# Layer-0 feed-forward of a two-layer ViT tower: tokens of seven quads turned by VectorE block transposes and DRAM transfers instead of PE transposes

## The chip, the core and the metric

The kernel runs on one core of one Trainium2 chip. The metric is the device time of one execution in microseconds (us); the time before is the median of three runs, 1921.87 us (1919.85 to 1925.09). The engines of the core are PE (matrix multiply), ACT, DVE (VectorE) and POOL (GpSimd). SP is a queue whose work here is to issue DMA transfers. Each engine works through its own instructions in order, and waits on semaphores for the others.

## What is computed

32 images of 256 tokens with 256 features, in float32, go through a tokenizer, a layer 0 (attention, then a feed-forward part that only half of the tokens get), and a layer 1. The change lies in the feed-forward part of layer 0, which in the reference, cut to what matters, is:

```python
def _L0_ffn_ref(x, attention_mask, wr, br, w1, b1, w2, b2):
    weights = (jnp.einsum('bsd,do->bso', x, wr) + br)[..., 0]
    k = max(1, int(CAPACITY * s))            # 128 of 256 tokens
    kk = k - 1 if k > 1 else 1               # 127 are processed
    _, idx = jax.lax.top_k(weights, k)
    sel_idx = idx[:, :kk]
    sel = jnp.take_along_axis(x, sel_idx[:, :, None], axis=1)
    h = jax.nn.gelu(jnp.einsum('bkd,dh->bkh', sel, w1) + b1)
    y = jnp.einsum('bkh,hd->bkd', h, w2) + b2
    ...
    processed = jnp.zeros_like(x).at[batch_idx, sel_idx].set(y)
    return processed + x
```

The product with `w1` sums over the features, so PE needs the selected tokens with features on the partitions. They arrive with tokens on the partitions; somebody has to turn them.

## The kernel before

The program is one long stream, stage after stage: tokenizer (A), layer-0 attention by pairs of images (B), layer-0 feed-forward by quads, that is four images (C), layer-1 attention by pairs (D), layer-1 feed-forward by images (E). In A to D the order of instructions on each engine is written by hand: what the Python loop calls first is first in every engine's queue. No scheduler moves anything there.

During B the tokens of each image are ranked and scattered by rank to DRAM (`ranked`, line 401, indirect DMAs of POOL). Stage C handles eight quads u = 0 to 7 in steps t, four steps to a quad. `ORDER_C` (line 857) says at which step, relative to t = 4u, each piece of quad u is called; within one step the pieces are called in the order of the tuple, whichever quad they belong to:

- `first_ranks` (line 220, step -8): four DMAs of SP load the first 128 ranked tokens of each image into `cs`, tokens on the partitions, 128 x 4 x 256. There are two `cs` buffers.
- `turn_c` (line 225, step -1): 8 PE transposes of 128x128 by the identity (line 230) into two PSUM banks, which ACT (k = 0, line 194) and DVE (k = 1, line 196) copy to `xsel`, 128 x 2 x 512, features on the partitions. There is one `xsel` buffer.
- `hidden_c` (line 814, steps 0 and 1): 16 matmuls of 512 columns from `xsel`, in two halves, with the Gelu on ACT (line 821). Float32 matmuls show in the trace as two instructions each, so 32 for a quad.
- `made` (line 823, steps 2 and 3): per half, 16 matmuls of 256 columns (32 in the trace), for two images; DVE adds the bias for each image (line 829, `cy`), and SP stores the result to DRAM (line 830, `results`).
- `fetch` (line 832, steps 4 and 5) is POOL's indirect DMAs from `results`; `update` (line 843, steps 5 and 6) adds on DVE (line 849) and takes statistics (lines 124 and 125).

So around the end of quad u-1 the calls run: step 4u-2: `made` of quad u-1, first half; `update` of quad u-2, second half. Step 4u-1: `turn_c` of quad u; `made` of quad u-1, second half. Step 4u: `hidden_c` of quad u. The weight products of `prepare()` (from line 630), one piece at the end of each step from t = 8, are set between these; they put PE work into some steps and none into others. Quad 0 is turned by a direct call of `turn_c` at the end of stage B (line 536).

All PE matmuls go through one helper and have line 116 in the profile; transposes of `turn_c` have line 230.

Of the kernel before, what the change touches and what calls it, by code (L numbers as in the profile page):

```python
# [33 lines left out]
F32 = mybir.dt.float32  # L34
# [6 lines left out]
P = 128  # L41
# [39 lines left out]
def vit_tower(tc, a, out):  # L81

    nc = tc.nc
# [13 lines left out]
    def bank():  # L97
        return ppool.tile([P, 512], F32, name="bank", tag="bank")

    def col(name, i=0):  # L100
        c = COLS[name][0] + i
        return cols[:, c : c + 1]
# [12 lines left out]
    def mm(o, lhsT, rhs, first=True, last=True):  # L115
        nc.tensor.matmul(o, lhsT, rhs, start=first, stop=last)  # L116
# [4 lines left out]
    def stats(st, i, c, x):  # L121

        six = spool.tile([P, 6], F32, name="six")
        nc.vector.bn_stats(six, x)  # L124
        nc.vector.bn_aggr(st[:, i, c, :], six)
# [26 lines left out]
    def pow_rstd_of(pair, b, images):  # L152
        st, rs, i = at(pair, b)
        q = slice(i * NC, (i + images) * NC)
        pow_rstd(rs[:, q], st.rearrange("p i c s -> p (i c) s")[:, q, 1])

    def new_stats(name):
        return [
            (
                cpool.tile([P, HALF, NC, 2], F32, name=f"st_{name}{k}", tag=f"st{k}", bufs=2),  # L160
                cpool.tile([P, HALF * NC], F32, name=f"rs_{name}{k}", tag=f"rs{k}", bufs=2),
            )
            for k in range(2)
        ]

    def at(pair, b):

        st, rs = pair[b // HALF]
        return st, rs, b % HALF
# [22 lines left out]
    def copy_split(k, o, i):  # L192
        if k == 0:
            nc.scalar.copy(o, i)
        else:
            nc.vector.tensor_copy(o, i)
# [6 lines left out]
    px = passing_x.enter_context(tc.tile_pool(name="c_x", bufs=1, reuse_waits="tile"))  # L203
    pdram = passing_x.enter_context(tc.tile_pool(name="c_d", bufs=1, space=bass.MemoryType.DRAM))
# [8 lines left out]
    p0 = region_c0.enter_context(tc.tile_pool(name="c_0", bufs=1, reuse_waits="tile"))  # L213
# [11 lines left out]
    def turn_c(b0, s, _):  # L225
        s.xsel = p0.tile([P, 2, 4 * P], F32, name="xsel")
        for k in range(2):
            p = bank()
            for j in range(4):
                nc.tensor.transpose(p[:, j * P : (j + 1) * P], s.x[:, j, k * P : (k + 1) * P], ident)  # L230
            copy_split(k, s.xsel[:, k, :], p)

    wpool = region.enter_context(tc.tile_pool(name="w_c", bufs=1))
    region_b = ExitStack()
# [38 lines left out]
    with (  # L273
# [7 lines left out]
        for k, n in enumerate(PARTS):  # L281
            f = sum(PARTS[:k])
# [5 lines left out]
        p = bank()  # L288
# [116 lines left out]
    with (  # L405
# [71 lines left out]
        def turn_weights(b0):  # L477
            p = bank()
            for j in range(2):
                w = normed_c[b0][j][1]  # L480
                for c in range(NC):
                    o = j * N + c * P
                    nc.tensor.transpose(p[:, o : o + P], w[:, c : c + 1].to_broadcast([P, P]), ident)  # L483
            return p

        def ranks(b0, p):
            for j in range(2):
                rank_c(b0 + j, *normed_c[b0][j], p[:, j * N : (j + 1) * N])

        def norms_c(b0):  # L490
            normed_c[b0] = [norm_c(b0 + j) for j in range(2)]

        def residuals_c(b0):
            for j in range(2):
                residual_c(b0 + j, normed_c[b0][j][0])
# [6 lines left out]
        for t in range(B // 2 + 2):  # L502
# [30 lines left out]
            if older:  # L533
                gated_b(*older)
                if t == B // 2 + 1:
                    turn_c(0, quads[0], 0)
                    norms_c(2 * (t - 3))
                    residuals_c(2 * (t - 3))
                output_b(*older)
# [77 lines left out]
    for i in range(2):  # L617
        s, t = slice(i * HD, (i + 1) * HD), slice((1 - i) * HD, (2 - i) * HD)
# [170 lines left out]
    def norm_d(b0, s, pool, name, bufs):  # L789
        s.xs = []  # L790
        for j in range(2):
            x = pool.tile([P, NC, D], F32, name=name, bufs=bufs)
            st, rs, i = at(st_d, b0 + j)
            q = slice(i * NC, (i + 1) * NC)
            one = spool.tile([P, NC], F32, name="d_one")
            nc.vector.scalar_tensor_tensor(one, st[:, i, :, 0], -1.0, rs[:, q], ALU.mult, ALU.mult)
            nc.vector.tensor_scalar(one, one, 1.0, None, ALU.add)
            for c in range(NC):
                nc.vector.tensor_scalar(
                    x[:, c, :], H[b0 + j][:, c, :], rs[:, i * NC + c : i * NC + c + 1], one[:, c : c + 1],  # L800
                    ALU.mult, ALU.add,
                )
            s.xs.append(x)
# [7 lines left out]
    with region_c:  # L811
        st_d = new_stats("d")

        def hidden_c(b0, s, half):
            if half == 0:
                s.hT = p2.tile([P, 8, 4 * P], F32, name="hT")
            for m in range(4 * half, 4 * half + 4):
                p = bank()
                for k in range(2):
                    mm(p, w1[:, k, m * P : (m + 1) * P], s.xsel[:, k, :], k == 0, k == 1)  # L820
                nc.scalar.activation(s.hT[:, m, :], p, AF.Gelu_apprx_tanh, bias=col("b1", m))

        def made(b0, s, half):
            for j in range(2 * half, 2 * half + 2):
                p = bank()
                for m in range(8):
                    mm(p[:, 0:D], s.hT[:, m, j * P : (j + 1) * P], w2[:, m, :], m == 0, m == 7)
                y = p2.tile([P, D], F32, name="cy", bufs=4)
                nc.vector.tensor_tensor(y, p[:, 0:D], row_c("b2"), ALU.add)
                nc.sync.dma_start(results[b0 + j][:], y)  # L830

        def fetch(b0, s, half):
            s.y = s.y if half else []
            for b in range(b0 + 2 * half, b0 + 2 * half + 2):
                y = px.tile([P, NC, D], F32, name="cx", bufs=8)
                for c in range(NC):
                    k = b * NC + c
                    nc.gpsimd.indirect_dma_start(
                        y[:, c, :], None, results[b][:], bass.IndirectOffsetOnAxis(rank_of[:, k : k + 1], 0)
                    )  # L840
                s.y.append(y)

        def update(b0, s, half):
            for j in range(2 * half, 2 * half + 2):
                b = b0 + j
                st, rs, i = at(st_d, b)
                for c in range(NC):
                    k = b * NC + c
                    nc.vector.scalar_tensor_tensor(  # L849
                        H[b][:, c, :], s.y[j][:, c, :], w_kept[:, k : k + 1], H[b][:, c, :], ALU.mult, ALU.add  # L850
                    )
                    stats(st, i, c, H[b][:, c, :])
            pow_rstd_of(st_d, b0 + 2 * half, 2)

        ORDER_C = ((0, hidden_c, 0), (1, hidden_c, 1), (2, made, 0), (-1, turn_c, 0), (-8, first_ranks, 0),
                   (3, made, 1), (4, fetch, 0), (5, fetch, 1), (5, update, 0), (6, update, 1))

        def step_c(t):  # L860
            for at_step, do, j in ORDER_C:
                u, r = divmod(t - at_step, 4)
                if r == 0 and 0 <= u < B // 4 and (u > 1 or do is not first_ranks):
                    do(4 * u, quads[u], j)

        END_C = 4 * (B // 4 - 1) + 4
        pairs = [Pair() for _ in range(B // 2)]
        preparing = prepare()
        for t in range(END_C):
            if t == 0:  # L870
                norms_c(B - 2)
                residuals_c(B - 2)
            if t == END_C - 2:
                for u in range(2):
                    norm_d(2 * u, pairs[u], px, "cx", 8)
            step_c(t)
            if t < 2:
                ranks(B - 4 + 2 * t, turn_weights(B - 4 + 2 * t))
            if t >= 8:
                next(preparing, None)  # L880
        passing.close()
# [5 lines left out]
    with (  # L887
# [100 lines left out]
        for t in range(3 * (NP - 1) + 8):  # L988
            def do(step, which, *more):
                u, r = divmod(t - step, 3)  # L990
                if r == 0 and 0 <= u < NP:
                    which(2 * u, pairs[u], *more)
# [41 lines left out]
    with (  # L1034
# [452 lines left out]
        p = bank()  # L1487
# [381 lines left out]
```

## Time and profile before

| what | value |
|---|---|
| median of three runs | 1921.87 us |
| the profiled execution's own time | 1921.73 us |
| its span in the profile | 1919.9 us |
| PE busy | 1876.7 us, 98% of the span |
| DVE, ACT, POOL busy | 1255.8, 814.9, 757.3 us |
| stage C on PE (first `xsel` matmul to last `hT` matmul) | 691.6 to 928.3 us |
| PE transposes of `cs` (line 230) | 64 instructions, 1.04 us for each quad's eight |
| copies to `xsel` in stage C | 585 ns (ACT), 678 ns (DVE) each, median |
| mean granted PE clock | 0.987 of full speed |

The page names for every group of instructions its line, its engine, what it writes and reads, how many there are, the busy time and the mean of one. "PEclk" is the clock that PE was granted. A DMA is listed with the time from its issue on the queue to its landing. The timeline gives start and duration in us.

### The profile page before, as it was taken

To read this page: it belongs to the slowest core of one execution; us is meant where nothing else is said; L and a number is where in the kernel's file an instruction comes from. 1 tells how busy PE (TensorE), PEld (TensorE's weight loads), DVE (VectorE), ACT (ScalarE), POOL (GpSimd) and SP (SyncE) were. 2 spreads that over 40 slices of the span, in tenths; PEclk is the share of its full clock that TensorE was granted. 3 is DMA by queue.
4 is the path that set the end of the run, shared out by engine and by line. 5 is a ranking of instruction groups with operands and counts; after the bars stand their busy time and mean duration, and the time that the engine had idled before them with its cause. 6 is when DMAs were issued, how large, how long until landed. Compare 5 with 4: busy or idle time off the path is not lost.

```text
span 1919.9 us, 36937 instructions
## 1 busy us (share of the span) xinstructions
PE 1876.7 (98%) x14852; PEld 1337.1 (70%) x14852; DVE 1255.8 (65%) x3257; ACT 814.9 (42%) x1646; POOL 757.3 (39%) x792
## 2 busy tenths in 40 slices
PE   9999999999999999999999999999999999999993
PEld 8887666666666676766655555568878878787872
DVE  2334456565657573434366556544999999999988
ACT  0001322222222212122343444447787888878772
POOL 1224223333343344334253333334454545455453
PEclk9999999999999999999999999999999999999995
DMA  9450000000000132222000000001222222222212
GB/s 306 152 150 15 1 17 25 25 17 17 15 19 14 41 113 83 61 75 63 12 22 1 1 1 1 1 13 24 60 54 63 57 57 63 52 62 57 63 40 57
DMA packets 69506, 94.49 MB, mean 49 GB/s; under 512 B 8656, under 2 KB 51152, under 8 KB 68944
## 3 DMA queue, kind: packets, MB, share of 16 engines
q1 hardware_dynamic: 62608, 74.49, 13.6%
q0 software_dynamic: 6144, 16.79, 2.8%
q8 instruction: 119, 1.95, 0.4%
q10 hardware_dynamic: 576, 0.79, 0.1%
q14 instruction: 59, 0.48, 0.1%
HBM read 46.41 MB, written 20.97 MB: 35 GB/s over the span
## 4 chain that ended last, share of the span: by engine, by line
PE 95%; DVE 4%; issue 0%; DMA 0%; ACT 0%; POOL 0%; SPq 0%; DVEq 0%; ACTq 0%
PE bank L116 91%; PE bank L772 2%; PE bank L189 1%; DMA patch<-in_patches_dram 0%; PE bank L230 0%; PE bank L483 0%; DVE six L124 0%; DVE fout L1367 0%; DVE fout L1381 0%; DVE eo L1245 0%; DVE ranges L1268 0%; DVE six L967 0%; DVE fout L1370 0%; DVE h L849 0%; DVE ey L1330 0%
## 5 line engine op out<-in xcount | busy, mean ns | idle before, releaser
L1164 POOL TENSOR_SCALAR_AFFINE_SELECT et<-et 128x512 f32<-128x512 f32 (+1 forms) x192 | 165.7, 875 | 203.3 <-ACT et L1155 201.3
L1155 ACT ACTIVATE et<-bank 128x512 f32<-128x512 f32 x384 | 207.7, 630 | 30.6 <-PE bank L116 30.3
L116 PE MATMUL bank<-ev,et 128*64 128x68 f32 (+1 forms) x6144 | 200.6, 226 | 0.0
L116 PEld LDWEIGHTS bank<-ev,et 128*64 128x64 f32 x6144 | 193.1, 138 | 5.7 <-issue 4.7
L116 PE MATMUL bank<-g,sx 64*128 64x512 f32 (+1 forms) x512 | 177.6, 486 | 0.0
L116 PE MATMUL bank<-g,sw 64*128 64x512 f32 (+1 forms) x512 | 177.2, 486 | 0.0
L116 PE MATMUL bank<-tokW,patch 128*128 128x256 f32 x768 | 168.0, 382 | 1.7 <-DMA patch<-in_patches_dram 1.7
L116 PEld LDWEIGHTS bank<-tokW,patch 128*128 128x128 f32 x768 | 146.8, 191 | 23.2 <-issue 2.7
L116 PE MATMUL bank<-bxT,w_wuv 128*128 128x512 f32 x300 | 131.4, 592 | 0.0
L1184 ACT COPY eo<-bank 128x280 f32<-128x280 f32 x256 | 96.1, 395 | 70.1 <-PE bank L116 62.8
L116 PEld LDWEIGHTS bank<-g,sx 64*128 64x128 f32 x512 | 93.1, 187 | 31.8 <-issue 22.9
L116 PE MATMUL bank<-wvo,dm 128*128 128x512 f32 x256 | 114.3, 599 | 0.0
L116 PE MATMUL bank<-attn,bv 128*128 128x256 f32 x512 | 113.1, 379 | 0.0
L116 PE MATMUL bank<-w_wo,gT 128*128 128x256 f32 x512 | 113.1, 379 | 0.0
L116 PE MATMUL bank<-w_w,hT 128*128 128x256 f32 x512 | 113.1, 379 | 0.0
L116 PE MATMUL bank<-xsel,w_w 128*128 128x512 f32 x256 | 111.4, 592 | 0.0
L116 PEld LDWEIGHTS bank<-attn,bv 128*128 128x128 f32 x512 | 97.2, 190 | 19.6 <-issue 6.9
L124 DVE BATCH_NORM_STATS2 six<-h 128x6 f32<-128x256 f32 x256 | 105.5, 412 | 4.4
L116 PEld LDWEIGHTS bank<-w_w,hT 128*128 128x128 f32 x512 | 96.6, 190 | 15.3 <-issue 2.9
L116 PEld LDWEIGHTS bank<-g,sw 64*128 64x128 f32 x512 | 93.1, 187 | 20.1 <-issue 9.9
L116 PEld LDWEIGHTS bank<-w_wo,gT 128*128 128x128 f32 x512 | 97.2, 190 | 13.2
L116 PE MATMUL bank<-w_wuv,bxT 128*128 128x512 f32 x240 | 105.4, 592 | 0.0
(275 smaller groups left out, 3688.8 us busy)
## 6 DMA issues: line engine op xcount, KB each, us to landing
patch<-in_patches_dram SPq DMA_DIRECT2D x31, 768.0 KB, 4.8
sw<-sx SPq DMA_DIRECT2D x64, 128.0 KB, 2.4
out_dram<-fout SPq DMA_DIRECT2D x32, 256.0 KB, 2.7
both<-fxT SPq DMA_DIRECT2D x62, 128.0 KB, 2.3
both<-hx SPq DMA_DIRECT2D x62, 128.0 KB, 2.3
cs<-ranked SPq DMA_DIRECT2D x32, 128.0 KB, 3.0
results<-cy SPq DMA_DIRECT2D x32, 128.0 KB, 1.7
w_w<-in_w_dram SPq DMA_DIRECT2D x2, 1024.0 KB, 8.3
```

Of the source, the lines that this page charges most:

```text
L116: nc.tensor.matmul(o, lhsT, rhs, start=first, stop=last)
L124: nc.vector.bn_stats(six, x)
L189: nc.tensor.transpose(p[:, o : o + P], x[:, c, k * P : (k + 1) * P], ident)
L772: nc.tensor.transpose(p[:, o : o + P], x[:, c, k * P : (k + 1) * P], ident)
L1155: nc.scalar.activation(t2[:, i, :], p, AF.Exp)
L1164: nc.gpsimd.affine_select(out=own, in_=own, pattern=[[0, 2 * n_e], [1, P]], compare_op=ALU.is_ge, fill=0.0, base=0, channel_multiplier=-1,)
L1184: nc.scalar.copy(im.o[:, g * OC : (g + 1) * OC], p[:, 0:OC])
```

## The change

For quads 1 to 7 `turn_c` is replaced by two pieces, both at step -2, that is one step earlier; quad 0 keeps `turn_c`.

```diff
+    def blocks_c(b0, s, _):
+        s.d = pdram.tile([32, 8 * 4, 4, 32], F32, name="c_turned", bufs=2)
+        y = px.tile([P, 8, 4, 32], F32, name="c_blocks", bufs=1)
+        nc.vector.transpose(y.rearrange("p f j t -> p j f t"), s.x.rearrange("p j (f t) -> p j f t", t=32))
+        for i in range(4):
+            nc.sync.dma_start(s.d[:, :, i, :], y[32 * i : 32 * i + 32].rearrange("p f j t -> p (f j) t"))
+
+    def turned_c(b0, s, _):
+        s.xsel = p0.tile([P, 2, 4 * P], F32, name="xsel")
+        d = s.d.rearrange("q (k f j) i p -> f q k (j i p)", k=2, f=4)
+        for f in range(4):
+            nc.sync.dma_start(s.xsel[32 * f : 32 * f + 32], d[f])
...
-        ORDER_C = ((0, hidden_c, 0), (1, hidden_c, 1), (2, made, 0), (-1, turn_c, 0), (-8, first_ranks, 0),
+        ORDER_C = ((0, hidden_c, 0), (1, hidden_c, 1), (2, made, 0), (-2, blocks_c, 0), (-2, turned_c, 0), (-8, first_ranks, 0),
                    (3, made, 1), (4, fetch, 0), (5, fetch, 1), (5, update, 0), (6, update, 1))
```

One DVE instruction turns every 32x32 block of `cs` within its own 32 partitions. Each of four DMAs then stores 32 partitions to a scratch in DRAM, in pieces of 32 floats (128 bytes), 1024 pieces in a DMA, since the pieces of the four groups of partitions alternate there. Each of four further DMAs reads 32 partitions of `xsel` back, in pieces of 512 floats (2 KB), 64 in a DMA. All eight are issued by SP. The built program has, per quad, the order: SP: results of the first half of `made`, four stores, four loads, results of the second half; DVE: two `cy` additions, the block transpose, then the second half of the `update` of quad u-2. The first load waits for all four stores to land, and for PE to be done with the old `xsel`.

## The prediction, written before the changed kernel was run

> **What bounds the kernel now.** I read the page first, then the chain of work around stage C, then PE's timeline there.
>
> ```profile
> span 1919.9 us, 36937 instructions
> ...
> PE   9999999999999999999999999999999999999993
> ...
> PE 95%; DVE 4%; issue 0%; DMA 0%; ACT 0%; POOL 0%; SPq 0%; DVEq 0%; ACTq 0%
> ```
>
> PE is busy in every slice but the last and is 95% of the chain that ended last. So time on PE is time of the kernel, and a moment in which PE waits is added in full. The chain between 680 and 935 us (start, length, what) shows what the turning costs now:
>
> ```profile
> 836.12 0.87 PE bank L230 x8
> 836.99 27.55 PE bank L116 x96
> 864.54 0.87 PE bank L230 x8
> ```
>
> The eight transposes of a quad are 0.87 us of the chain, and one quad's turn is 28.42 us long. The copies to `xsel` are not in the chain. PE's timeline (start, length) says how much work lies between the place where the new pieces are called and the place where `xsel` is needed:
>
> ```profile
> 835.95 1.04 PE L230 MATMUL bank<-ident,cs 128*128 128x128 f32 x8
> 836.83 7.07 PE L116 MATMUL bank<-w_w,hT 128*128 128x256 f32 x32
> 843.73 13.90 PE L116 MATMUL bank<-xsel,w_w 128*128 128x512 f32 x32
> ```
>
> At 835.95 the first half of `made` ends on PE; call it zero. `hidden_c` starts at 7.78 us; without the transposes it could start at 7.78 - 0.87 = 6.91 us. That is the whole cover of the new path.
>
> **What it removes.** 7 quads x 0.87 us of PE on the chain: -6.1 us. The copies (7 on ACT, 585 ns; 7 on DVE, 678 ns) go too; both engines wait for PE in this stage, so I count nothing.
>
> **What it adds, as a chain from zero.** PE is in order and by hand: behind its wait for `xsel` stands everything else, so nothing else can fill the gap.
>
> 1. DVE gets free. The block transpose stands behind the two `cy` additions, and the second one can't run before `made` ends. DVE's timeline:
>
> ```profile
> 836.15 0.42 DVE L829 TENSOR_TENSOR cy<-bank,rows_c 128x256 f32<-128x256 f32 x1 [3.03 <-PE bank L116]
> 836.49 0.47 DVE L849 SCALAR_TENSOR_TENSOR h<-cx,w_kept,h 128x256 f32<-128x256 f32 x1
> ```
>
> The next instruction starts at 836.49, so the transpose starts at 0.54 us.
>
> 2. The transpose, 128x1024 float32. The trace has no such operation. Rows of that size (mean ns behind the comma):
>
> ```profile
> L927 DVE TENSOR_TENSOR dz<-dz,dn 128x1024 f32<-128x1024 f32 x16 | 19.6, 1226 | 0.5
> L926 DVE TENSOR_SCALAR dn<-dz 128x1024 f32<-128x1024 f32 x16 | 11.1, 694 | 0.6
> ```
>
> 0.69 is the lower end; the dearest row of this size (line 1245, 2618 ns) the upper one. I take 1.23, the row without a faster mode: done at 1.77. The DVE work behind it moves back by 1.23 less the 0.68 of the copy that goes. It is the `update` of quad u-2, which nobody on PE waits for in this stage; cost nothing.
>
> 3. Issue on SP. Four loads to `cs` take 1.83 us of the queue together, 0.46 each. First store at 1.87 with 0.1 for the wait.
>
> 4. The four stores, 4096 pieces of 128 bytes, 256 for each of 16 DMA engines. A result store was issued at 738.74 and the DMA engines began to move 0.8 us later (the fifteenth of 40 slices in the DMA view of 738.5 to 741.5); so the first byte moves at 2.67. The price of a piece is the large unknown. No transfer of the trace has many pieces of 128 bytes, so I bound it by two windows of the DMA view (packets, MB, share of 16 engines): the small loads of 256 bytes between 703.7 and 708.0 us, and one result store of 1 KB pieces between 738.5 and 741.5 us.
>
> ```profile
> q1 hardware_dynamic: 480, 0.10, 11.0%
> ```
> ```profile
> q1 hardware_dynamic: 144, 0.13, 12.9%
> ```
>
> The first: 0.110 x 16 x 4.3 us / 480 = 15.8 ns a piece. The second: 0.129 x 16 x 3.0 us / 144 = 43 ns. In size the new pieces are nearer the first, in direction (a store to DRAM) nearer the second. I take the middle, 30 ns: 256 x 0.030 = 7.7 us. Ends: 4.0 and 11.0 us; outside them, 1.5 us if only bytes counted (1 KB in 48 ns at the 341 GB/s of 12 to 20 us), and 17.1 us at the queue's mean over the kernel (13.6% of 16 x 1919.9 us over 62608 packets = 66.7 ns). That result store moved until 740.08 and landed 1.7 us after its issue, at 740.44, so 0.36 is for the receipt. All landed at 2.67 + 7.7 + 0.36 = 10.73.
>
> [...]
>
> 5. The four loads wait on SP for all four stores: 0.1. Issue 3 x 0.46 = 1.37 until the last one goes out, and then it lands as `cs<-ranked` does, four at a time as well:
>
> ```profile
> DMA to landing us min/median/max: 1.9/3.0/4.4
> ```
>
> So `xsel` is there at 10.73 + 0.1 + 1.37 + 3.0 = 15.2.
>
> 6. PE's stall: 15.2 - 6.9 = 8.3 us a quad. Seven quads: 58.1. Two quads have more cover, since pieces of `prepare` fall into it: before quad 3, 773.57 to 775.71 and 783.62 to 784.64 (3.1 us); before quad 4, 805.37 to 805.80 and 813.59 to 815.31 (2.2 us). 58.1 - 5.3 = 52.8.
>
> 7. PE's clock after a stall. Windows near the end (PEclk is the third number from the right) and the same 32 matmuls before and after a wait of 3.61 us:
>
> ```profile
> 1838.00:1840.00 2.00, 0.97 (x16) 0.84 (x18) 2.00 (x2) 0.31 (x1) 1.83 (x2) 1.00 0.00 0
> 1840.00:1842.00 2.00, 2.00 (x44) 2.00 (x42) 1.30 (x3) 2.00 (x6) 0.00 (x0) 0.54 0.19 44
> 1842.00:1844.00 2.00, 2.00 (x37) 1.92 (x34) 1.24 (x2) 0.67 (x3) 0.00 (x0) 0.61 0.42 92
> ```
> ```profile
> 1866.26 1.17 PE L116 MATMUL bank<-W,both 128*64 128x68 f32 x32
> 1878.66 2.46 PE L116 MATMUL bank<-W,both 128*64 128x68 f32 x32 [3.61 <-ACT hv L1275]
> ```
>
> After a wait of 2.07 us the granted clock lost 0.46 x 2 + 0.39 x 2 = 1.7 us of work. I add that for each of seven stalls: 11.9 us. Ends: 0, and 3.4 us if it takes twice as long to come back.
>
> Behind the loads on SP stand the results of `made`'s second half; `fetch` needs them at step 4u+1, 7 us into `hidden_c`, and they are issued before `hidden_c` starts. `update` waits for those, and the `cy` additions of the next quad stand behind it 14 us later. Nothing.
>
> **The sum.** -6.1 + 52.8 + 11.9 = +58.6. The profiled execution took 1921.73 (span 1919.9 and 1.8 around it), 0.1 below the median: **1980 us**.
>
> **The rivals.**
>
> - *Hidden, and so faster.* If `xsel` is there within 6.9 us, only the -6.1 is left: 1915.6. This decides at the landing of the loads: with the fastest of all rows (0.69 for the transpose, byte price only with the fastest result landing, 1.7, and 1.9 for a load) it comes at 0.54 + 0.69 + 0.1 + 1.4 + 1.7 + 0.1 + 1.4 + 1.9 = 7.8. Every row would have to be beaten. For it: the pieces are spread over idle DMA engines (share 0.24 in the windows of 800 to 860 us). Chance 0.03.
> - *Latency only.* The pieces cost hardly more than bytes; the stall is 0.9 us by the fastest landings and up to 4.6 at 15.8 ns. At 0.9, 5 x 0.9 - 6.1 gives 1920; at 15.8 ns, 25 us below the forecast, 1955. For it: DMA busy shares are low. Against: even whole 1 KB pieces take 43 ns. Chance 0.14.
> - *Dearer pieces.* At 66.7 ns the stores take 9.4 us more a quad, 66 us in all: 2046; dearer still beyond it. For it: the 1024 pieces of a DMA go into DRAM 512 bytes apart, which nothing here does. Chance 0.17.
> - *It does not do what it says.* The built order has the pieces where the change puts them, on the queues it names; only if PE already waited there for something else would the stall cost nothing, and its timeline has no gap. Chance 0.01 (1922).
> - *Forecast*, 15.8 to 43 ns: 1955 to 2003, around 1980. Chance 0.65.
>
> **The numbers.** The range leaves out the hidden case, about half of the latency case and the far half of the dear one: 1935 to 2046. A measurement tells about 0.3% from no change, here 5.8 us. Faster by more than that: the hidden case, 0.03. Within it: the bottom of the latency case and the last rival, 0.04. Slower: 0.93.
>
> **What would show it.** PE should wait for a DMA to `xsel` seven times, about 8 us each (about 5 and 6 before quads 3 and 4), where it waited for nothing; the transposes of line 230 should drop from 64 to 8; the four stores should take 8 to 9 us from first issue to last landing, and the granted clock should fall below 1.00 in the windows behind each stall. If the stores land in 4 us, step 4 was too dear; if PE has no wait there, step 1 to 6 are wrong as a whole. The stages before and after C should keep their lengths to a microsecond.

## The result, and the profile after

The changed kernel takes 1966.05 us (median of 4 runs, 1961.14 to 1969.55) against 1922.47 for the kernel before (4 runs): 1.0227 of its time, 95% interval 1.0204 to 1.025, that is 43.6 us slower. The profiled execution took 1965.92 us, its span is 1964.2.

From the page of the changed kernel, the lines that answer to those of before:

```profile
span 1964.2 us, 36896 instructions
...
PE   9999999999999988988898999999999999999993
...
PEclk9999999999999989989999999999999999999995
...
PE 91%; DVE 4%; DMA 3%; SPq 1%; ACT 1%; issue 1%; POOL 0%; DVEq 0%; ACTq 0%
```

Six slices of PE in stage C have fallen to 8, the clock has in two (the last slice, with its 5, is the end of the program, not stage C), and DMA and SP's queue are in the chain that ended last with 3% and 1%, where they stood at 0%. PE's waits, summed up (us, times, longest), name who is waited for:

```profile
PE bank L116 <- DMA xsel<-c_turned: 35.4, 7, 7.1
```

And PE's timeline around quad 5 (start, length, then in brackets the idle time and what ended it):

```profile
853.81 13.98 PE L116 MATMUL bank<-w_w,hT 128*128 128x256 f32 x64
873.54 16.99 PE L116 MATMUL bank<-xsel,w_w 128*128 128x512 f32 x32 [5.76 <-DMA xsel<-c_turned]
890.37 13.98 PE L116 MATMUL bank<-w_w,hT 128*128 128x256 f32 x64
```

Two losses stand there. PE is idle for 5.76 us, and then `hidden_c`, which took 13.90 us before, takes 16.99. Both happen seven times. The windows of that stretch (PEclk is the third number from the right) show why the second comes:

```profile
853.00:873.00 20.00, 14.78 (x67) 12.30 (x65) 7.75 (x20) 0.69 (x1) 5.05 (x6) 0.99 0.39 90
873.00:882.00 9.00, 8.46 (x13) 3.67 (x14) 3.28 (x9) 1.39 (x3) 5.06 (x7) 0.63 0.53 153
882.00:890.00 8.00, 8.00 (x20) 3.48 (x19) 0.00 (x0) 3.42 (x5) 0.00 (x0) 1.00 0.00 0
```

The mean granted clock of the 9 us around PE's return is 0.63. In finer windows, shown at the last experiment, it falls to 0.50 at 872.8, shortly before the wait ends, and is 1.00 again from 879.7, so that the first 6.1 us of `hidden_c` run at half speed.

The chain from the end of the first half of `made` can be followed on DVE and SP:

```profile
860.91 0.42 DVE L842 TENSOR_TENSOR cy<-bank,rows_c 128x256 f32<-128x256 f32 x1 [3.03 <-PE bank L116]
861.25 1.24 DVE L236 STREAM_TRANSPOSE c_blocks<-cs 128x1024 f32<-128x1024 f32 x1
...
862.52 2.76 SPq L238 DMA_DIRECT2D c_turned<-c_blocks  x4
...
867.49 2.49 SPq L244 DMA_DIRECT2D xsel<-c_turned  x4
```

4.97 us lie between the first store and the first load (the loads wait for all stores), and 6.05 us between the first load and PE's return at 873.54.

Stage C, from its first `xsel` matmul to the first transpose of stage D (us), shows where the time is in every run of this study. "Wait" is PE's waits for `xsel` (seven, in e3 six); "empty" is PE time in matmuls that an experiment added (0.43 us each); "slow" is what the seven `hidden_c` took beyond 13.90 each.

| kernel | median, us | ratio to before (95%) | stage C | wait | empty | slow |
|---|---|---|---|---|---|---|
| before | 1919.45 to 1922.47, by group of runs | 1 | 236.5 | 0 | 0 | 0.1 |
| after | 1966.05 | 1.0227 (1.0204 to 1.025) | 284.4 | 35.4 | 0 | 17.5 |
| e1_warm | 1952.2 | 1.0153 (1.0137 to 1.0169) | 266.9 | 4.6 | 30.1 | 0.5 |
| e2_early | 1915.23 | 0.9964 (0.9951 to 0.9978) | 230.4 | 0 | 0 | 0.1 |
| e3_whole_pieces | 1936.65 | 1.0086 (1.0063 to 1.0108) | 246.9 | 15.0 | 0 | 0.5 |
| e4_stores_early | 1914.08 | 0.9960 (0.9945 to 0.9975) | 230.4 | 0 | 0 | 0.1 |
| e5_results_last | 1958.89 | 1.0205 (1.0188 to 1.0222) | 272.8 | 28.6 | 0 | 12.7 |
| e6_two_queues | 1956.05 | 1.0184 (1.0167 to 1.0201) | 273.5 | 28.5 | 0 | 13.5 |
| e7_short_idle | 1960.96 | 1.0215 (1.0198 to 1.0232) | 273.9 | 18.8 | 16.8 | 6.7 |

The columns add up: 236.5 less 6.1 for the missing transposes is 230.4; for the changed kernel 230.4 + 35.4 + 17.5 = 283.3 of 284.4. The rest, about 1.1 in every kernel that waits, is seven times the tail of the last matmul, which otherwise lies under the next one (0.16 us: at quad 5 of the changed kernel `hidden_c` starts at 873.54 and takes 16.99, and the next group starts at 890.37). What follows stage C takes 988.3 to 993.6 us in the profiles of all nine kernels, with the same code; a difference of a few us between two single profiles is not the change.

### The profile page after: what moved, and what is told of

Same layout as the page of the kernel before. It is cut to its first block, busy times and chain, and to the rows that moved or that the text cites. A ratio compares the mean times of both kernels' runs of the same rounds, so it can differ in the third digit from the quotient of the medians.

```text
span 1964.2 us, 36896 instructions
## 1 busy us (share of the span) xinstructions
PE 1885.2 (96%) x14796; PEld 1334.3 (68%) x14796; DVE 1262.3 (64%) x3257; ACT 810.7 (41%) x1639; POOL 756.5 (39%) x792
## 4 chain that ended last, share of the span: by engine, by line
PE 91%; DVE 4%; DMA 3%; SPq 1%; ACT 1%; issue 1%; POOL 0%; DVEq 0%; ACTq 0%
PE bank L116 88%; PE bank L785 2%; DMA xsel<-c_turned 1%; PE bank L189 1%; SPq L244 1%; DMA c_turned<-c_blocks 0%; DMA patch<-in_patches_dram 0%; PE bank L496 0%; DVE six L124 0%; ACT et L1168 0%; DVE fout L1380 0%; SPq L238 0%; DVE fout L1394 0%; DMA both<-hx 0%; DVE h L862 0%
## 5 line engine op out<-in xcount | busy, mean ns | idle before, releaser
L116 PE MATMUL bank<-xsel,w_w 128*128 128x512 f32 x256 | 128.9, 667 | 35.4 <-DMA xsel<-c_turned 35.4
L834 ACT ACTIVATE hT<-bank,cols 128x512 f32<-128x512 f32 x64 | 44.0, 687 | 220.6 <-PE bank L116 220.6
L116 PEld LDWEIGHTS bank<-xsel,w_w 128*128 128x128 f32 x256 | 54.2, 215 | 105.4 <-issue 104.9
```

## The experiments

The theory from this profile: what costs is the part of the chain (block transpose, four stores, four loads) that sticks out of its 6.9 us of PE cover, and with it the clock that PE loses while idle. The rivals: the added work costs by itself (traffic, SP's queue, DVE late for PE's results); or `hidden_c` is slow because of the transfers, not the clock.

**e1_warm: PE kept busy during the wait.** In `step_c`, ahead of `hidden_c`:

```diff
+                    if do is hidden_c and j == 0 and u:
+                        p = bank()
+                        for _ in range((0, 14, 12, 3, 6, 12, 12, 11)[u]):
+                            mm(p[:, 0:N], zero[:, 0:P], zero)
```

> In the changed kernel PE waits seven times for the loads of xsel (35.4 us in all), and the seven runs of hidden_c after these waits are 15.6 to 17.0 us long instead of 13.90, 17.5 us in all. Here PE does empty matmuls of zeros (0.43 us each, 3 to 14 of them by quad) inside those waits, so that it is never idle for much over a microsecond; their product is read by nobody. Theory (the extra 17.5 us is the clock that PE loses by idling): xsel arrives as before, PE's remaining waits plus the empty matmuls are again about 35 us, hidden_c goes back to 13.9 us, and the time falls by 12 to 18 us, to 1948 to 1954. Rival (hidden_c is longer because its first matmuls still wait for late loads, or because transfers disturb it): hidden_c stays at 15.6 to 17.0 and the time stays at 1963 to 1969.

Measured: 1952.2 us. PE's timeline at quad 5:

```profile
859.01 5.34 PE L116 MATMUL bank<-zero 128*128 128x256 f32 x24
865.32 13.97 PE L116 MATMUL bank<-xsel,w_w 128*128 128x512 f32 x32 [0.97 <-DMA xsel<-c_turned]
```

This lies in the range of the theory. Wait and empty matmuls together are 34.7 us, nearly the 35.4 of the wait in the changed kernel, and every `hidden_c` is back at 13.97. So the 17.5 us are PE's idling and nothing that the transfers do to it.

**e2_early: the same work with more cover.**

```diff
-                   (-2, blocks_c, 0), (-2, turned_c, 0),
+                   (-4, blocks_c, 0), (-3, turned_c, 0),
```

> Block transpose and stores are called at step -4 instead of -2, the loads at step -3 (after the last matmul that reads the old xsel); the work is the same in number and size. Theory (only the chain of transfers that sticks out of its 6.9 us of PE cover costs time): the chain gets more than 14 us of cover, PE waits for nothing, and what is left is the seven missing turns of 0.87 us on PE: 1922.5 - 6.1 = 1916.4, between 1913 and 1919. Rival (the added transfers and the block transposes cost by themselves, by traffic on the DMA engines, by SP's queue, or by DVE being late for the bias additions): the time stays above 1930, and the timeline shows the waits moved elsewhere.

Measured: 1915.23 us, 0.9964 of before, in the range of the theory. PE's timeline at quad 5 has no gap ahead of `xsel`:

```profile
824.48 13.98 PE L116 MATMUL bank<-w_w,hT 128*128 128x256 f32 x64
838.29 13.90 PE L116 MATMUL bank<-xsel,w_w 128*128 128x512 f32 x32
```

The same block transposes, stores and loads cost nothing here. This rules out that they cost by themselves, and leaves their place in the order.

**e3_whole_pieces: 32 pieces of 4 KB in a store in place of 1024 of 128 bytes.**

```diff
-        s.d = pdram.tile([32, 8 * 4, 4, 32], ...)
+        s.d = pdram.tile([32, 4, 8 * 4, 32], ...)
-            nc.sync.dma_start(s.d[:, :, i, :], ...)
+            nc.sync.dma_start(s.d[:, i, :, :], ...)
-        d = s.d.rearrange("q (k f j) i p -> f q k (j i p)", k=2, f=4)
+        d = s.d.rearrange("q i m t -> q (i m t)").rearrange("q (k f x) -> f q k x", k=2, f=4)
```

> Each store now writes one whole 4 KB piece per partition to the scratch (32 pieces in place of 1024), and the loads read 2 KB pieces as before; the values come back in another order, so tokens and features of quads 1 to 7 are mixed up, the work on every engine is the same. The prediction's step 4 had 7.7 us a quad for the 4096 small pieces. If the pieces were that dear, the stores would land 5 to 7 us earlier and the time would fall by 35 us or more, to below 1932. Theory after the profile of the changed kernel (11 to 12 ns a piece, mostly beside the issuing of the four stores, 0.69 us each): the last store lands 0.5 to 1.7 us earlier, and the time falls by 3 to 12 us, to 1954 to 1963.

Measured: 1936.65 us, 29 us less than the changed kernel (27 by the ratios): neither number held. SP's queue and PE's timeline at quad 5:

```profile
841.45 1.72 SPq L238 DMA_DIRECT2D c_turned<-c_blocks  x4
844.42 2.48 SPq L244 DMA_DIRECT2D xsel<-c_turned  x4
```
```profile
849.34 13.97 PE L116 MATMUL bank<-xsel,w_w 128*128 128x512 f32 x32 [2.62 <-DMA xsel<-c_turned]
```

First store to first load is 2.97 us instead of 4.97, and the loads themselves take 4.92 instead of 6.05. In the profile that took 20.4 us off PE's waits, and with waits of at most 3.2 us all of the lost clock came back, 17.0 us. The profiled execution is the fastest of four (1931.98; the others 1933.89 to 1942.5), and their granted clock falls with the time: 0.988 in the two fastest runs, 0.985 and 0.982 in the two slowest. That fits clock lost again in those two, but they have no trace. I had expected 0.5 to 1.7 us a quad from the stores, had not seen that the loads would gain too, and had left the clock out.

**e4_stores_early: only the stores are moved ahead.**

```diff
-                   (-2, blocks_c, 0), (-2, turned_c, 0),
+                   (-4, blocks_c, 0), (-2, turned_c, 0),
```

> Only block transpose and stores are moved, to step -4; the loads stay at step -2, behind the two result stores on SP. Theory: what sticks out is then only the wait of SP for the second bias addition (0.6 us after the end of the first half of made) and the loads, 6.0 us from first issue to the first matmul: 6.6 us against 6.9 us of cover, so PE waits 0 to 0.5 us a quad: 1916 to 1921. If instead the loads are most of the stall by themselves (their landing behind other traffic, or their wait for the old buffer), PE would still wait 3 us or more a quad: 1935 or more.

Measured: 1914.08 us, 0.9960 of before, 2 us below the lower end of the expectation, since PE does not wait at all. From the end of the first half of `made` (half of the matmuls before quad 5, 825.27 + 6.91 = 832.18), the loads are issued at 1.1 us and PE goes on without a gap:

```profile
833.26 2.50 SPq L244 DMA_DIRECT2D xsel<-c_turned  x4
```
```profile
839.09 13.90 PE L116 MATMUL bank<-xsel,w_w 128*128 128x512 f32 x32
```

The loads alone (here 5.8 us at most from issue to use) fit under the cover. Transpose and stores are what did not. The intervals of e2 and e4 lie below 1 and overlap; both are faster than before.

**e5_results_last: are the loads delayed by their neighbours?** The two stores of `results` of the first half move behind the loads:

```diff
-                nc.sync.dma_start(results[b0 + j][:], y)
+                if half == 0:
+                    s.kept_y = (s.kept_y if j else []) + [y]
+                else:
+                    nc.sync.dma_start(results[b0 + j][:], y)
...
+        def store_made(b0, s, _):
+            for j in range(2):
+                nc.sync.dma_start(results[b0 + j][:], s.kept_y[j])
...
-                   (-2, turned_c, 0), (-8, first_ranks, 0),
+                   (-2, turned_c, 0), (2, store_made, 0), (-8, first_ranks, 0),
```

> The changed kernel, but the two result stores of the first half of made are issued behind the loads of xsel, so that they and the fetches that wait for them come after the loads. In the changed kernel the loads landed a median 3.5 us after their issue and PE went on 6.05 us after the first of them was issued; where the loads came before the fetches (whole pieces) or far from the stores (stores early) it was 3.0 and 4.9 us. Theory (fetches and result stores share the DMA engines with the loads and delay them by about 1 us): the loads land in 3.0 us, PE's seven waits fall by 0.8 to 1.2 us each to about 28 us, and the time falls by 5 to 9 us, to 1957 to 1961. Rival (the loads are late by themselves, because they read what was just stored in small pieces): landing stays at 3.5, the time stays at 1963 to 1969.

Measured: 1958.89 us. SP, POOL and PE at quad 5:

```profile
860.78 2.49 SPq L244 DMA_DIRECT2D xsel<-c_turned  x4
```
```profile
866.78 1.06 POOL L858 DMA_INDIRECT cx<-results,rank_of  x1 [5.28 <-DMA results<-cy]
```
```profile
865.86 15.65 PE L116 MATMUL bank<-xsel,w_w 128*128 128x512 f32 x32 [4.62 <-DMA xsel<-c_turned]
```

First load to PE's return is 5.08 us instead of 6.05, and the first fetch now goes out after PE is back. The waits fell by 6.8 us as expected. So about 1 us of each wait was other DMA work in the same moments: the fetches, which in the changed kernel began at 868.23, 0.7 us behind the first load, and the result stores. Which of the two weighs more was not taken apart.

**e6_two_queues: every second store and load issued by ACT.**

```diff
-            nc.sync.dma_start(s.d[:, :, i, :], ...)
+            (nc.sync, nc.scalar)[i % 2].dma_start(s.d[:, :, i, :], ...)
-            nc.sync.dma_start(s.xsel[32 * f : 32 * f + 32], d[f])
+            (nc.sync, nc.scalar)[f % 2].dma_start(s.xsel[32 * f : 32 * f + 32], d[f])
```

> The changed kernel, but every second store and every second load is issued by ACT's queue instead of SP's; ACT has nothing to do in these moments and its next work waits for xsel in any case. Theory (the queue's issue, 0.69 us a store and 0.62 a load one after the other, is about half of the stall): the last store goes out 1.4 us earlier and the last load another 1.2, PE waits 2.6 us less a quad (16 to 20 us in all instead of 35.4), most waits become shorter than the 3.2 us after which the whole-piece run lost no clock, so most of the 17.5 us of slow hidden_c go too: 1928 to 1942. Rival (the DMA engines, not the queue, set the pace of stores and loads): the waits shorten by less than 1 us each, and the time stays above 1955.

Measured: 1956.05 us, above 1955 as the rival said, with waits 1.0 us shorter each (28.5 us in all); the theory of the queue fell for the stores. The DMA view of e6 from the first store to the first load, 855.8 to 860.6 us (40 slices of the DMA engines' busy tenths, then packets, MB and share by queue):

```profile
DMA  4000000000499999999996999999999995000000
...
q1 hardware_dynamic: 2120, 0.29, 35.5%
q10 hardware_dynamic: 2080, 0.26, 33.3%
```

and of the changed kernel, from 862.5 to 867.5 us:

```profile
DMA  6000000000699999999998999996999992000000
...
q1 hardware_dynamic: 4214, 0.56, 63.5%
```

In both, the DMA engines are busy without a break for about 24 of 40 slices, 2.9 us: 256 pieces an engine on average, 11 ns each. Two queues do not shorten that; first store to first load stayed at 4.9 us. The loads gained 0.8 us at quad 5 (860.64 to 865.86 is 5.2 us).

**e7_short_idle: how long a wait costs the clock?** As e1, with fewer empty matmuls:

```diff
-                        for _ in range((0, 14, 12, 3, 6, 12, 12, 11)[u]):
+                        for _ in range((0, 10, 7, 0, 2, 7, 7, 6)[u]):
```

> As the run with empty matmuls in the wait, but fewer of them (10, 7, 0, 2, 7, 7, 6 before quads 1 to 7), so that PE is left idle about 2 to 3 us each time. Theory (the clock falls only when PE is idle for some 3.3 us or more; the whole-piece run kept it at waits of 2.6 to 3.2 us): hidden_c of quads 1, 2, 4, 5, 6, 7 stays at 13.9 to 14.0 us; quad 3, whose wait of 1.94 us is as in the changed kernel and follows matmuls of 4 to 16 columns, is slow again at about 17 us; the time is 1950 to 1958. Rival (any wait of 2 us or more costs the clock, and the whole-piece run was luck of the phase): most hidden_c are 15.6 to 17 us, and the time is 1960 to 1968.

Measured: 1960.96 us, above the theory's range and just inside the rival's. Lines of PE's timeline at quads 2, 5 and 7:

```profile
762.42 15.38 PE L116 MATMUL bank<-xsel,w_w 128*128 128x512 f32 x32 [2.86 <-DMA xsel<-c_turned]
...
869.02 13.97 PE L116 MATMUL bank<-xsel,w_w 128*128 128x512 f32 x32 [2.75 <-DMA xsel<-c_turned]
...
935.98 15.64 PE L116 MATMUL bank<-xsel,w_w 128*128 128x512 f32 x32 [2.95 <-DMA xsel<-c_turned]
```

After waits of nearly one length `hidden_c` is 1.5, 0.1 and 1.7 us longer than 13.90. Four of the seven `hidden_c` were slow (15.4 to 15.7 us) and three were not: the theory fell, and the rival's "any wait of 2 us or more" holds for four of seven. Quad 3, which the theory had slow, was not. Over all runs with a wait: every wait of 3.4 us or more was followed by a `hidden_c` 1.6 to 3.1 us longer (16 of 16), none of up to 1.0 us was (8 of 8), and between 1.1 and 3.2 us it went both ways (9 of 17).

What decides it stands in the same traces, in the moments at which the granted clock changes. The changed kernel from the start of the wait at quad 5 to the end of `hidden_c` (PEclk is again the third number from the right):

```profile
867.78:872.80 5.02, 0.00 (x1) 0.00 (x0) 1.46 (x4) 0.00 (x0) 3.92 (x5) 1.00 0.72 183
872.85:879.60 6.75, 6.06 (x7) 2.53 (x8) 3.29 (x10) 0.69 (x1) 4.33 (x7) 0.50 0.66 192
879.70:890.50 10.80, 10.80 (x27) 4.82 (x26) 0.00 (x0) 4.12 (x6) 0.78 (x1) 1.00 0.05 12
```

The clock is whole for the first 5 us of the wait, and changes at 872.8 and 879.65. Its other changes nearby, at 838.65, 842.1, 906.95 and 913.75, lie on one raster with these: the distances are 1, 9, 2, 8 and 2 times 3.41 us. In e5, e6 and e7 all changes of stage C lie on such a raster as well, within 0.05 us, each run with its own phase (in e7, by start of `hidden_c` and twice its loss against 13.97, the clock is whole again at 765.24 and 836.92, 21 times 3.41 us apart). If the waits are laid over it (in e1 and e3, which lose no clock in stage C, the raster is continued back from changes after it, an estimate), 22 of the 25 slow `hidden_c` come after a stretch of the raster with 2.03 us or more of wait in it (the least at quad 4 of e7), and none of the 16 others had more than 1.98 us in one stretch (the most at quad 6 of e7). The three exceptions are quad 3 of the changed kernel, e5 and e6: 1.0 to 1.2 us of wait, next to 1.2 us of matmuls with 4 to 16 columns. So the rival's other half was right, as far as that estimate goes: by it the waits of 2.6 to 3.2 us in e3 were each cut in two by the raster, with at most 1.86 us on one side, which is a matter of phase.

## Why the prediction was right, and where its sizes were not

The mechanism was the forecast one, the sign and the range held; 1980 was 14 us too high. That it came so near is partly luck. The pieces cost 11 ns, outside the 15.8 to 43 ns on which the forecast case rested and in the region of the case "latency only", which had a chance of 0.14; with 11 ns alone put right, the sum would have given 1947, 19 us too low. The loads, the receipt and the clock, all counted too cheap, made up for it. By its steps:

- **What goes** (-6.1): right. With the new path covered, stage C of e2 and e4 is 236.5 - 230.4 = 6.1 us shorter, and the kernels are 6 to 7 us faster. Line 230 has 8 transposes left of 64.
- **Steps 1 and 2**, DVE free at 0.54 and 1.23 for the transpose: right. It starts 0.53 us after PE's end (860.72) and takes 1234 ns; the 1226 ns row was the right one. That the 694 ns row had a faster mode was my reading; the rows show their times alone.
- **Step 3**, 0.46 us of issue each: 0.69 for the stores and 0.62 for the loads at quad 5. For the stores the issue cost nothing (first store to first load at quad 5: 4.97 us, and 4.86 with two queues in e6).
- **Step 4, the term that failed**: 30 ns for a piece, 7.7 us a quad. The pieces took 11 ns, 2.9 us, less even than the 15.8 ns of the 256-byte row, which I had taken for the lower end. From first issue to the first load, which waits for the last landing, it was 4.97 us and not 8 to 9. First move (1.2 us after issue instead of 0.8) and receipt (about 0.8 us from the last move to the first load, instead of 0.36 and 0.1) took 0.8 us more than I had counted. By the balance of sizes and directions I took a middle; the row nearest in size came closer, and that the pieces are stores did not make them dearer than that row.
- **Step 5**, 4.4 us for the loads: 6.05, of which e5 traces 1 us to other transfers and 0.5 is the longer issue. That other DMA work runs beside the loads stood nowhere in the sum.
- **Step 6**, 52.8 us of waits: 35.4. The cover of quads 3 and 4 was seen right: their waits are 1.94 and 3.43 us, the others 5.4 to 7.1.
- **Step 7**, 11.9 us for the clock: 17.5. In quads 2, 4 and 6 `hidden_c` lost 1.7 to 1.8 us, as counted; in quads 1, 3, 5 and 7 it lost 2.9 to 3.1, since 5.8 to 6.3 us of their work fell into the half clock, close to the upper end of 3.4 us lost that was given. The sum had one loss for all waits; in the traces the clock changed on the raster of 3.41 us, and, quad 3 aside, the smallest wait within one stretch of it ahead of a slow `hidden_c` was 2.03 us (quad 4 of e7).

So -6.1 + 35.4 + 17.5 = 46.8, against a forecast of 58.6; stage C grew by 47.9, the profiled execution by 44.2, the medians by 43.6.

The hidden case, that I gave 3 in 100, needs the landing within 6.9 us; it came at 12.8 (873.54 less 860.72). e2 shows that this point decides: more than 6 us of further cover, and the time is below that of before.

## What to carry to other kernels

Work taken off the engine that bounds a kernel is a gain only if what replaces it ends under cover: 0.9964 and 0.9960 of the time before with it (e2, e4), 1.0227 without. Count the cover from the instruction that the new chain is queued behind, here the second bias addition, not from where it would be free to start: the block transpose needed nothing from `made`, and two steps earlier the same change is a gain. To a wait of PE add the clock that it costs, half as much again here (17.5 us on 35.4).

## What was not expected of the hardware

- The four stores of a quad, in 4096 pieces of 128 bytes, moved at 11 ns a piece and engine, about 180 GB/s in all, with one issuing queue (changed kernel) or two (e6), both at quad 5.
- Such a store took 0.67 us on the issuing queue (median of 28, changed kernel), one of the same bytes in 32 pieces 0.41 us (e3).
- After a wait of PE of 1.1 to 3.2 us, 9 of 17 `hidden_c` had lost 1.5 us or more (one of them 3.1). The length of the wait did not tell which; how a raster of 3.41 us cut the wait did, all but quad 3, with 2.03 us or more of wait within one stretch where clock was lost and at most 1.98 us where it was not. Why `hidden_c` was also slow at quad 3 of three runs, after 1.0 to 1.2 us of wait beside small matmuls, was not tested.
